# Adding a small constant inside the mask multiplication and not in a pass of its own

## The chip, the cores and the metric

The kernel runs on one core of a Trainium2 chip. Of the engines of the core, TensorE does the matrix products, ScalarE (ACT in the profile) applies functions element by element, VectorE (DVE) does arithmetic on one or two tensors, GpSimd (POOL) does some of the additions, and SyncE (SP) issues nearly all transfers. The metric is the device time of one execution in microseconds (us), the median over several runs.

## The reference

Sixty-four graphs of 256 nodes with 512 features each go through an attention layer with 8 heads and then a graph-attention block with two more attentions. The adjacency matrix `adj` (256 x 256 for each graph) holds edge weights between 0.05 and 1, and zero where there is no edge (about 97 in 100 entries; the diagonal is always set). It enters three times:

```python
# layer 0, 8 heads
scores = Q K^T / sqrt(64) + soul_bias + log(adjacency + 1e-9)
out = softmax(scores) V + x
# layer 1, first 8 heads, then one head
e = leaky_relu(s_i + t_j, 0.2) + bias          # bias is the same adjacency
out = softmax(e) h + x
```

In layer 0, exp(log(a + 1e-9) + z) is (a + 1e-9) exp(z). So the logarithm needs not be taken: the exponentials of the scores are multiplied by the adjacency plus the constant. In layer 1 the adjacency is added to the scores as it is.

## The kernel before

**Layout.** All attention matrices are held turned: a partition is a source node j, and the columns are the target nodes. So the adjacency of a graph is turned first. `turn_adj` in `graph` does it with two VectorE transposes of 128x256 (line 501, called for each half j), from the tile `A` as loaded into `AT`, 128 partitions by 2 x 256 columns. Then one ScalarE pass over the whole of `AT` (128x512, line 517) adds `eps`, a column of 1e-9:

```python
nc.scalar.activation(AT, AT, AF.Identity, bias=eps)
```

**Where `AT` is read.** Layer 0: after the exponentials of the scores (line 599, ScalarE, straight from PSUM into `ET`), VectorE multiplies them by `AT` (line 613). For each graph there are four such passes of 128x1024, for two groups of four heads and the two halves j; `AT` is broadcast over the four heads. After each group of heads the two halves are summed (line 618, `total`), and TensorE sums the columns of the totals for the softmax denominators (line 384 in `weight_sums`). Layer 1, first attention: `AT` is added to the scores (line 682) between two ScalarE passes (lines 676 and 686). Layer 1, last attention: `AT` goes through an exponential in place (line 739) and is a factor in line 744. `AT` has four buffers, since several graphs are under way at once.

**Projections.** Products of 512 features are done by a scheme with seven block products in place of eight, in `winograd` (lines 326 and 333 are its matmuls). They use three PSUM banks, a, b and c, over and over: `m1` is copied out of a and `m5` out of b, then products 2 and 6 follow, then `u2` is copied out of a, products 3, 7 and 4 follow. So a product that goes into bank a again has to wait until the copy of what lay there is done. For K these copies are ScalarE passes (line 525, `m<-ps_a`, `m<-ps_b`, `u<-ps_a` of 128x256).

**Order of the work.** A graph is a generator of 40 or so steps with names ("turn", "Q", "K", "K7", "mask", "weights" and so on). The list `period` says in which order the steps of up to six graphs are taken, and it repeats for each graph; a `start` and a `finish` list stand around it. For TensorE this order is kept as written:

```python
with tc.manual_schedule(engines={mybir.EngineType.PE}):
```

The order of the other engines is left to the framework's planner, which starts from the program order and its own costs. In `period` the steps around the turning are these (the number is how many graphs back):

```python
(0, "turn"), (1, "Q4"), (1, "K"), (1, "K7"), (3, "weights"),
```

At the end a check of the value ranges decides whether a slow, plain path has to be run for some graphs (the loop over `again`); with the inputs here it is not run. It has its own code for the constant and is not touched.

Of the kernel before, what the change touches and what calls it, by code (L numbers as in the profile page):

```python
# [10 lines left out]
AF = mybir.ActivationFunctionType  # L11
ALU = mybir.AluOpType
AX = mybir.AxisListType

P = 128
# [5 lines left out]
def kernel(  # L21
# [24 lines left out]
    nc = tc.nc  # L46
    B, N, D = x.shape
# [11 lines left out]
    eps = const.tile([P, 1], F32, name="eps")  # L59
# [92 lines left out]
    with ExitStack() as main:  # L152
# [324 lines left out]
        def graph(b):  # L477
# [22 lines left out]
            def turn(to, blocks):  # L500
                nc.vector.transpose(to, blocks)
# [7 lines left out]
            AT = data.tile([P, NT, N], F32, name="AT", tag="AT", bufs=4)  # L509

            def turn_adj():
                for j in range(NT):
                    turn(
                        AT[:, j, :].rearrange("p (t a r) -> p a t r", t=NT, a=4),
                        A.rearrange("p (a t) (j r) -> p j a t r", t=NT, j=NT)[:, j],
                    )
                nc.scalar.activation(AT, AT, AF.Identity, bias=eps)

            if b > 0:
                turn_adj()  # L520
# [21 lines left out]
            if b == 0:  # L542
                turn_adj()
# [66 lines left out]
            totals = []  # L610
            for ET, tag in zip(pair, ("QT", "KT")):
                for j in range(NT):
                    nc.vector.tensor_tensor(  # L613
                        ET[:, j, :, :], ET[:, j, :, :],
                        AT[:, j, :].unsqueeze(1).to_broadcast([P, 4, N]), ALU.mult,
                    )
                total = data.tile([P, 4, N], F32, name="total", tag=tag)
                nc.vector.tensor_tensor(total, ET[:, 0], ET[:, 1], ALU.add)
                totals.append(total)
                yield  # L620
# [49 lines left out]
            for q in range(2):  # L670
                ET = work.tile([P, NT, 4, N], F32, name="ET1", tag="ET", bufs=4)
                pair.append(ET)
                for h in range(4):
# [5 lines left out]
                    if h % 2 == 1:  # L679
                        for j in range(NT):  # L680
# [4 lines left out]
                            for i in (h - 1, h):  # L685
                                nc.scalar.activation(  # L686
                                    ET[:, j, i, :], ET[:, j, i, :], AF.Exp,
                                    bias=targets[:, j, 4 * q + i : 4 * q + i + 1],
# [53 lines left out]
            ET = work.tile([P, NT, N], F32, name="ET2", tag="ET2", bufs=1)  # L742
# [115 lines left out]
        graphs = {}  # L858
        with tc.manual_schedule(engines={mybir.EngineType.PE}):
            graphs[0] = graph(0)  # L860
            next(graphs[0])
            wv, wq, wk = weight("wv", 1), weight("wq"), weight("wk")
# [22 lines left out]
            for g, name in order:  # L885
                for key, (behind, t, w) in list(unloaded.items()):
                    if (g, name) == (key, "transpose") or behind in graphs:
                        load_weight(nc.sync, t, w)
                        del unloaded[key]
                if (g, name) == (0, "Q"):  # L890
                    nc.vector.tensor_scalar(wq[:, :, :4], wq[:, :, :4], SCALE, None, ALU.mult)
                    combine(wq)
                if (g, name) == (0, "K"):
                    combine(wk)
                if (g, name) != (0, "load"):
                    if g not in graphs:
                        graphs[g] = graph(g)
                    next(graphs[g])
                if (g, name) == (B - 1, "rows 2"):

                    note_odd(seen[:, : 4 * B], -1.0, 1e25)
                    note_odd(seen[:, 4 * B :], -1.0, 3600.0)
# [13 lines left out]
    with ExitStack() as rest:  # L916
# [6 lines left out]
        def tl(name, *shape):  # L923
            return pool.tile(list(shape), F32, name=name, tag=name)
# [108 lines left out]
        with tc.For_i(0, again) as b:  # L1033
# [8 lines left out]
            eps = tl("eps", P, 1)  # L1042
# [82 lines left out]
```

## Time and profile before

| | |
|---|---|
| median of 3 runs | 3233.33 us (3231.98 to 3235.2) |
| profiled execution, its own time | 3234.22 us |
| its span in the profile | 3232.4 us |
| granted TensorE clock, mean | 0.991 |
| DMA traffic | 407.94 MB, mean 126 GB/s |
| one period (from one L517 to the next, steady stretch) | 48.3 to 49.7 us mostly |

The span is what the profiler saw of the one execution; the execution's own time is 1.8 us longer. Busy shares are averages over the whole span, and the profile's slices show all engines at an even load from the second slice to the last but one. L517 means line 517 of the kernel. "ET<-ET,AT" says which tile is written from which. "x512" is a count. The time in brackets behind a line of the timeline is how long the engine sat idle before it, and what ended that. PE is TensorE's matmuls and PEld its loads of weights.

### The profile page before, as it was taken

Reading aid. Unit: us, or ns where it says so; the run is one execution under the profiler, and the core shown is the slowest. Engines: PE = TensorE matmul, PEld = TensorE weight load, DVE = VectorE, ACT = ScalarE, POOL = GpSimd, SP = SyncE. Lnnn points to the kernel's source line nnn. Section 1 sums busy time; section 2 is a strip of 40 time slices with the busy share of each in tenths; the row PEclk is TensorE's granted clock in tenths of the full one; section 3 lists DMA queues with packets and bytes.
Section 4 is the critical chain, followed back from the end, with each engine's and each line's share of the span. In section 5 each row is a group of like instructions: output and inputs, shape, how many; then the busy total and the mean of one; then the engine's idle time right before and its main releaser. Section 6 shows DMA issues by size and latency. Waiting matters only on the chain. (4 is left out here: it accounts for less than half of the span.)

```text
span 3232.4 us, 77827 instructions
## 1 busy us (share of the span) xinstructions
PE 3135.6 (97%) x28232; PEld 2621.6 (81%) x28232; DVE 2717.1 (84%) x6093; ACT 2188.5 (68%) x5959; POOL 1068.4 (33%) x1315
## 2 busy tenths in 40 slices
PE   7899999999999999999999999999999999999986
PEld 5678888888888888888888888888888888888864
DVE  5788888888888888888888888888888888888885
ACT  3467677677677677676676676676676676676673
POOL 3232332332332332333333333333323423423333
PEclk9999999999999999999999999999999999999998
DMA  4234444444444444444444444444444434444432
GB/s 133 92 118 131 124 131 131 126 127 133 127 128 133 127 124 135 128 122 134 129 122 136 125 126 124 131 130 125 132 124 132 132 123 133 131 123 133 125 116 90
DMA packets 354664, 407.94 MB, mean 126 GB/s; under 512 B 117840, under 2 KB 262496, under 8 KB 354272
## 3 DMA queue, kind: packets, MB, share of 16 engines
q1 hardware_dynamic: 353120, 401.83, 41.6%
q8 instruction: 224, 3.67, 0.5%
q14 instruction: 168, 1.38, 0.1%
q10 hardware_dynamic: 1152, 1.06, 0.1%
HBM read 266.83 MB, written 135.87 MB: 125 GB/s over the span
## 5 line engine op out<-in xcount | busy, mean ns | idle before, releaser
L682 DVE TENSOR_TENSOR ET<-ET,AT 128x512 f32<-128x512 f32 x512 | 363.4, 711 | 239.3 <-ACT ET L676 238.7
L686 ACT ACTIVATE ET<-ET,ends 128x256 f32<-128x256 f32 x1024 | 482.1, 503 | 104.7 <-DVE ET L682 103.6
L676 ACT ACTIVATE ET<-R,f 128x256 f32<-128x256 f32 x1024 | 461.3, 501 | 74.9 <-PE ps_num L425 55.7
L425 PE MATMUL ps_num<-ET,V 128*32 128x256 f32 x8192 | 466.7, 379 | 0.0
L302 POOL TENSOR_TENSOR S<-yT 128x256 f32<-128x256 f32 x64 | 47.7, 746 | 1210.5 <-ACT zT L409 967.6
L765 POOL TENSOR_TENSOR X<-X,weighted 128x256 f32<-128x256 f32 x256 | 210.9, 834 | 545.0 <-ACT weighted L764 536.9
L425 PEld LDWEIGHTS ps_num<-ET,V 128*32 128x32 f32 x8192 | 263.9, 110 | 155.2 <-issue 1.1
L613 DVE TENSOR_TENSOR ET<-ET,AT 128x1024 f32<-128x1024 f32 x256 | 306.6, 1231 | 39.4 <-ACT ET L599 39.4
L599 ACT ACTIVATE ET<-ps_sc,V 128x512 f32<-128x512 f32 x512 | 302.3, 697 | 7.8 <-PE ps_sc L592 7.8
L756 PE MATMUL ps_av<-V,ET 128*128 128x258 f32 (+1 forms) x1024 | 250.7, 389 | 24.3 <-DVE ET L744 24.3
L326 PE MATMUL ps_a<-w,S 128*128 128x264 f32 (+1 forms) x1024 | 268.5, 385 | 4.9 <-ACT m L639 2.9
L326 PE MATMUL ps_b<-w,S 128*128 128x264 f32 (+1 forms) x1024 | 266.6, 383 | 0.8 <-DVE w L131 0.7
L592 PE MATMUL ps_sc<-QT,KT 64*128 64x256 f32 x2048 | 239.4, 383 | 0.0
L263 DVE BATCH_NORM_STATS2 parts<-Z 128x6 f32<-128x128 f32 x1024 | 238.3, 275 | 0.1
L756 PEld LDWEIGHTS ps_av<-V,ET 128*128 128x128 f32 x1024 | 189.8, 196 | 48.9 <-issue 13.0
L326 PEld LDWEIGHTS ps_a<-w,S 128*128 128x128 f32 x1024 | 185.9, 189 | 46.7 <-ACT m L639 6.9
L326 PEld LDWEIGHTS ps_b<-w,S 128*128 128x128 f32 x1024 | 193.8, 189 | 32.5 <-PE ps_a L326 1.1
L592 PEld LDWEIGHTS ps_sc<-QT,KT 64*128 64x128 f32 x2048 | 192.4, 187 | 24.8 <-issue 1.5
L646 ACT ACTIVATE V<-ps_a,rstd 128x257 f32<-128x257 f32 (+1 forms) x128 | 60.0, 469 | 199.2 <-PE ps_a L326 199.2
L434 DVE TENSOR_TENSOR ps_num<-ps_num,R 128x512 f32<-128x512 f32 x256 | 169.9, 687 | 9.6 <-DMA R<-kept 7.0
L702 POOL TENSOR_TENSOR Z<-Z,bw 128x1024 f32<-128x1024 f32 x64 | 175.7, 2745 | 4.1 <-DVE parts L263 3.0
L409 ACT ACTIVATE yT<-yT,columns 128x256 f32<-128x256 f32 x256 | 120.8, 499 | 65.4 <-DMA yT<-kept 65.4
(175 smaller groups left out, 7396.3 us busy)
## 6 DMA issues: line engine op xcount, KB each, us to landing
R<-kept SPq DMA_DIRECT2D x128, 512.0 KB
X<-in_x_dram SPq DMA_DIRECT2D x256, 128.0 KB
kept<-xT SPq DMA_DIRECT2D x64, 512.0 KB
yT<-kept SPq DMA_DIRECT2D x64, 512.0 KB
R<-kept SPq DMA_DIRECT2D x512, 64.0 KB
kept<-yT SPq DMA_DIRECT2D x64, 512.0 KB
kept<-Z SPq DMA_DIRECT2D x64, 512.0 KB
X<-kept SPq DMA_DIRECT2D x512, 64.0 KB
```

The lines of the kernel that those rows point to most:

```text
L263: nc.vector.bn_stats(parts[:, block].rearrange("p h c -> p (h c)"), Z[:, block, :])
L326: nc.tensor.matmul(to, A[:, kk, :], B[:, kk, :], start=(first and kk == 0), stop=(kk == 1), skip_group_check=not first,)
L425: nc.tensor.matmul(num[32 * a : 32 * a + 32, m * N : (m + 1) * N], V[:, j, a // 2, a % 2 * P + q * DH + 32 * m :][:, :32], pair[a // 2][:, ...
L592: nc.tensor.matmul(banks[h % 2][:, o : o + N], KT[lo : lo + DH, (q + h) // 2, j * P : (j + 1) * P], QT[lo : lo + DH, (q + h) // 2, :], sta ...
L599: nc.scalar.activation(ET[:, j, i::2, :], banks[i].rearrange("p (h n) -> p h n", n=N), AF.Exp, bias=c[:, j, :],)
L613: nc.vector.tensor_tensor(ET[:, j, :, :], ET[:, j, :, :], AT[:, j, :].unsqueeze(1).to_broadcast([P, 4, N]), ALU.mult,)
L676: nc.scalar.activation(ET[:, j, h, :], R[q][:, h, :], AF.Relu, bias=f[:, j, at : at + 1])
L682: nc.vector.tensor_tensor(two, two, AT[:, j, :].unsqueeze(1).to_broadcast([P, 2, N]), ALU.add)
L686: nc.scalar.activation(ET[:, j, i, :], ET[:, j, i, :], AF.Exp, bias=targets[:, j, 4 * q + i : 4 * q + i + 1],)
L702: nc.gpsimd.tensor_tensor(Z, Z, folded["2"].row.unsqueeze(1).to_broadcast([P, 2 * KC, P]), ALU.add)
L756: nc.tensor.matmul(av[:, :width], ET[:, j, t * P : (t + 1) * P], V2[:, j, n, :width], start=(j == 0), stop=(j == NT - 1),)
L765: nc.gpsimd.tensor_tensor(o[:, cols], o[:, cols], weighted, ALU.add)
```

## The change

`turn_adj` no longer adds the constant; `AT` holds the adjacency as it was loaded, only turned. The four mask passes of layer 0 become a scalar-tensor-tensor with two operations: the constant 1e-9, given in the instruction, is added to `AT`, and the sum is multiplied by the exponentials. In layer 1 the adjacency is now used without the constant, as in the reference.

```diff
                         AT[:, j, :].rearrange("p (t a r) -> p a t r", t=NT, a=4),
                         A.rearrange("p (a t) (j r) -> p j a t r", t=NT, j=NT)[:, j],
                     )
-                nc.scalar.activation(AT, AT, AF.Identity, bias=eps)
 
             if b > 0:
                 turn_adj()
...
             for ET, tag in zip(pair, ("QT", "KT")):
                 for j in range(NT):
-                    nc.vector.tensor_tensor(
-                        ET[:, j, :, :], ET[:, j, :, :],
-                        AT[:, j, :].unsqueeze(1).to_broadcast([P, 4, N]), ALU.mult,
+                    nc.vector.scalar_tensor_tensor(
+                        ET[:, j, :, :], AT[:, j, :].unsqueeze(1).to_broadcast([P, 4, N]), 1e-9,
+                        ET[:, j, :, :], ALU.add, ALU.mult,
                     )
                 total = data.tile([P, 4, N], F32, name="total", tag=tag)
                 nc.vector.tensor_tensor(total, ET[:, 0], ET[:, 1], ALU.add)
```

## The prediction

> **What bounds the kernel now.** I read the engine totals first, then the waits of TensorE, then one period of each engine's timeline. The totals:
>
> ```profile
> PE 3135.6 (97%) x28232; PEld 2621.6 (81%) x28232; DVE 2717.1 (84%) x6093; ACT 2188.5 (68%) x5959; POOL 1068.4 (33%) x1315
> ```
>
> TensorE is busy throughout. The groups that it works through follow each other at a constant distance, so time can be lost or won only where that distance is larger than usual. Its waits outside the start and the end are few; the largest that recurs is one on a ScalarE copy:
>
> ```profile
> PE ps_av L756 <- DVE ET L744: 24.3, 4, 12.6
> PE ps_a L333 <- ACT m L525: 16.4, 27, 1.7
> ```
>
> The first of these is the tail (4 waits, up to 12.6 us). The second is the K projection of the middle of a period. ScalarE and TensorE there, from the timeline (start, length, and in brackets the idle time before):
>
> ```profile
> 1537.18 0.60 ACT L558 ACTIVATE QT<-ps_a,columns 128x128 f32<-128x128 f32 x2
> 1537.68 0.36 ACT L525 COPY m<-ps_a 128x256 f32<-128x256 f32 x1
> 1537.93 0.38 ACT L525 COPY m<-ps_b 128x256 f32<-128x256 f32 x1
> 1538.19 0.52 ACT L686 ACTIVATE ET<-ET,ends 128x256 f32<-128x256 f32 x1
> 1538.61 0.72 ACT L517 ACTIVATE AT<-AT,eps 128x512 f32<-128x512 f32 x1
> 1539.22 0.51 ACT L686 ACTIVATE ET<-ET,ends 128x256 f32<-128x256 f32 x1
> 1539.62 0.36 ACT L525 COPY u<-ps_a 128x256 f32<-128x256 f32 x1
> ```
>
> ```profile
> 1538.09 1.16 PE L333 MATMUL ps_a<-S,wk 128*128 128x128 f32 x8 [0.54 <-ACT m L525]
> 1539.08 1.06 PE L333 MATMUL ps_b<-S,wk 128*128 128x128 f32 x8
> 1540.03 1.16 PE L333 MATMUL ps_a<-S,wk 128*128 128x128 f32 x8
> ```
>
> The pass that goes (L517) stands behind both m copies and ahead of the u copy. I compared its neighbours in all 64 repeats: in the steady stretch they are these every time, about 48.3 to 49.7 us from one L517 to the next. So L517 cannot cause the wait on m; it can only hold up u, which product 7 (the third group above) needs.
>
> **What the Trainium skill says.**
> - "Perfetto Trace Analysis", section "Identifying the Most-Contended Engine": matmul busy time is no good measure of a full TensorE, because matmuls overlap; weight-load busy time is one. Here that is 81%, so I count distances between starts and not the 97%.
> - "ScalarE: Activation LUTs", "What ACT_TABLE_LOAD costs": a pass with a per-partition bias takes 280 ns + 0.833 ns per element, and neighbours overlap by about 93 ns. For 512 elements 707 ns; the trace has 720, and the next pass starts 0.61 us after L517. It agrees.
> - "VectorE: DVE Perf Modes", "The TRN2 errata": an fp32 tensor_tensor takes (N+151)/0.96 ns, for 1024 elements 1224; L613 has a median of 1225. It agrees.
> - "Vector Engine (DVE) Microarchitecture Reference", "Points that are easy to get wrong": a scalar-tensor-tensor with two non-bf16 SBUF sources runs at half throughput. The trace disagrees: L744 is such an instruction, and 256 elements take 474 ns, not over 530.
>
> **Removed.** 64 passes of L517: 46.1 us of ScalarE by the table of groups, about 64 x 0.61 = 39 us of its queue. What that is worth to TensorE:
> - Steady stretch. From product 3 to product 7 of K takes 1540.03 - 1539.08 = 0.95 us; the same step of Q (1527.28 to 1528.17) takes 0.89. I read it in 56 periods between 250 and 3000 us: 54 have 0.05 to 0.07 too much, and the sum is 3.5 us. Without L517 ScalarE reaches u at 1539.62 - 0.61 = 1539.01, but u then waits for product 6 (end 1538.09 + 1.16 = 1539.25). It would end near 1539.66, before product 3 has been fed (1539.08 + 0.89 = 1539.97). So all of the 0.06 goes: 57 x 0.06 = 3.4 us. Lower end 0, if another pass (L676, step 0.40) fills the gap. The rest of the 0.61 us is worth nothing: ScalarE idles again at 1543.03 and 1545.36 for TensorE and VectorE, which is where it is absorbed.
> - Start. Twice TensorE waits on a copy that stands behind L517, which itself waits for the turning on VectorE:
>
> ```profile
> 44.12 1.14 PE L326 MATMUL ps_a<-wv,S 128*128 128x257 f32 x4 [1.14 <-ACT u L525]
> 97.20 1.16 PE L326 MATMUL ps_a<-w,S 128*128 128x264 f32 x4 [1.43 <-ACT u L639]
> ```
>
>   The first 1.14 us is given back at 68.81, where TensorE waits 3.51 us for the folded weights, which start on GpSimd at 61.46 after 20.2 us that the profile puts down to issue and not to TensorE. After the second, the next group waits on V (L648), at 98.40 on VectorE. It stands behind L537, which ends its turn at about 98.2; so 0.2 us is left of 1.43. I take 0.2, ends 0 and 2.5.
>
> **Added.** Each of the 256 mask passes (L613) becomes a scalar-tensor-tensor with an immediate, over the same 1024 elements. No such pass of that size is in the trace. The prices that bound it:
>
> ```profile
> L613 DVE TENSOR_TENSOR ET<-ET,AT x256: 1206/1225/1792, 38.9 to 3120.9; 128x1024 f32<-128x1024 f32 x128
> L744 DVE SCALAR_TENSOR_TENSOR ET<-R,f,AT x126: 466/474/947, 221.6 to 3202.3; 128x256 f32<-128x256 f32 x126
> L374 DVE SCALAR_TENSOR_TENSOR bad<-seen 128x256 f32<-128x256 f32 x2 | 0.8, 414 | 0.0
> L374 DVE SCALAR_TENSOR_TENSOR bad<-seen 128x128 f32<-128x128 f32 x2 | 0.6, 281 | 0.0
> ```
>
> L374 takes an immediate: (414-281)/128 = 1.04 ns per element and 148 ns fixed, so 1024 elements give about 1214 ns, 11 less than L613. L744, whose scalar is a column, costs 474-414 = 60 more. At two elements the form with an immediate (L288) and the plain one (L289) both average 149. I take +-0; ends -11 and +60, and 1067 more if the halving did apply.
>
> This price matters, because the mask chain is tight. VectorE starts it at 1511.08, does six passes (four L613, two L618) and ends at 1518.15; TensorE's column sums (L384) start at 1518.27. The same 0.11 to 0.14 us lies between the two in 58 of 63 periods. A wake-up takes 0.05 (m ends 1538.04, TensorE starts 1538.09), so the slack is about 0.075 us: 19 ns per pass. Beyond it each ns costs 4 x 57 = 0.23 us. At +60: 57 x (0.24 - 0.075) = 9.4 us. At -11 at most 57 x 0.044 = 2.5 us is won. GpSimd is idle from 1511.4 to 1530, so it does not disturb the passes.
>
> **Moved.** AT's last writer is now VectorE's turning. L613 and L682 follow it on their own engine, and L739 comes a whole period later, so no wait is added; no DMA is touched. Only TensorE's order is written by hand. The trace shows passes of the other engines out of program order (L409 between the L367s at 1520 to 1522), so the planner may arrange ScalarE and VectorE anew around the hole.
>
> **Sum.** The profiled execution took 3234.2 us (span 3232.4), 0.9 above the median. 3.4 + 0.2 = 3.6 us less is 3230.6 profiled, 3229.7 at the median; with 0.7 of the 2.5 that shorter masks could give I say 3229. This case's own range: 3225 (3.4 + 2.5 + 2.5 won) to 3233 (nothing won).
>
> **Rivals.** Two thousandths are 6.5 us, about what a measurement of this kernel can tell from no change.
> - *Likeliest, 0.49*: the order holds and only u profits. 0.33 of this within the bound, 0.16 faster than it, when the small gains add up.
> - *The wait on m shrinks, 0.22*: it loses 25.2 us over 57 periods above the usual distance, of which 57 x 0.09 = 5 come with any such change of group; 20 can be had. If the planner moves a pair of L686 behind m, half of it goes: 3233.3 - 3.6 - 12 = about 3218; all of it, 3210. For: an emptier ScalarE. Against: 26 late arrivals of R (18.9 us of ScalarE waiting for the DMA) seem to start this wait, and they do not change.
> - *A pass in front of m, 0.19, slower*: the new order puts one more L676 or L686 (0.40 us) ahead of the m copy, and TensorE waits that much longer in each period: 57 x 0.40 - 3.6 = 19 more, 3252; in half of the periods 3241. It decides from (6.5 + 3.6)/57 = 0.18 us per period on. For: this copy already has no slack in most periods. Against: the hole comes after m, and ScalarE is idle again 4 us later.
> - *The new pass is longer, 0.08*: +60 ns gives 3229.7 + 9.4 = 3239 (0.04, inside the bound); above 63 ns it is slower than the bound, and at half throughput 57 x (4.27 - 0.075) = 239 more, near 3470 (0.04). Against: L744 and L374.
> - *Nothing moves, 0.02*: the freed time is hidden, 3233.
>
> **Range and chances.** Faster 0.16 + 0.22 = 0.38; within 0.33 + 0.04 + 0.02 = 0.39; slower 0.19 + 0.04 = 0.23. From 3215 to 3243: below lies about a third of the second case (0.07), above half of the third (0.10) and the long masks (0.03). The tail, 3140 us on, waits for chains on VectorE and DMA; I count no gain there.
>
> **What would show it.** ScalarE's busy time falls by 46 us to about 2142; L613 stays at 1214 to 1235 ns; product 3 to 7 of K takes 0.89; the waits at 44 and 97 us are gone and the one at 68.8 is longer. I am wrong if the ScalarE order around K differs, if the wait on m changes by more than 5 us in sum, or if L384 gains a wait on L618.

## The result and the profile after

| | before | after |
|---|---|---|
| median of 11 runs each, us | 3235.2 (3231.45 to 3241.38) | 3245.76 (3239.05 to 3251.89) |
| ratio, 95% interval | | 1.0034 (1.0026 to 1.0041) |
| span of the profiled execution, us | 3232.4 | 3243.9 |
| granted TensorE clock | 0.991 | 0.991 |

The kernel became 10.6 us slower, where 4 us faster was forecast. The 64 passes are gone all the same. The engine totals of the changed kernel:

```profile
PE 3140.4 (97%) x28232; PEld 2621.1 (81%) x28232; DVE 2720.0 (84%) x6093; ACT 2153.9 (66%) x5895; POOL 1067.7 (33%) x1315
```

ScalarE has 64 instructions less and 34.6 us less busy time. From here on, lines behind 517 stand one lower than before (L613 is now L612, and so on). The mask pass in its new form, from the view by tile (shortest/median/longest in ns):

```profile
L612 DVE SCALAR_TENSOR_TENSOR ET<-AT,ET x256: 1207/1225/1785, 39.3 to 3131.0; 128x1024 f32<-128x1024 f32 x128
```

Its median is the 1225 ns of the plain multiplication, so the added form costs no more than the old one. Where time is lost is seen in the waits of TensorE:

```profile
PEld ps_a L333 <- ACT m L524: 27.1, 45, 2.0
PE ps_a L333 <- ACT m L524: 17.9, 27, 1.8
PEld ps_a L333 <- ACT u L524: 15.8, 59, 0.3
```

The columns are total us, number of waits, longest. The two waits on m are those of before, hardly changed (24.8 and 16.4 us then). The third is new: 59 times, once in nearly every period, TensorE waits up to 0.3 us for the copy of u. The same place on ScalarE and on TensorE, from the timeline of the changed kernel (L675 are Relu passes and L685 Exp passes, two of each for every head, one for each half j; the three groups of TensorE are products 6, 3 and 7):

```profile
1542.16 0.36 ACT L524 COPY m<-ps_a 128x256 f32<-128x256 f32 x1
1542.41 0.38 ACT L524 COPY m<-ps_b 128x256 f32<-128x256 f32 x1
1542.68 0.92 ACT L685 ACTIVATE ET<-ET,ends 128x256 f32<-128x256 f32 x2
1543.49 0.91 ACT L675 ACTIVATE ET<-R,f 128x256 f32<-128x256 f32 x2
1544.28 0.36 ACT L524 COPY u<-ps_a 128x256 f32<-128x256 f32 x1
```

```profile
1542.57 1.16 PE L333 MATMUL ps_a<-S,wk 128*128 128x128 f32 x8 [1.28 <-ACT m L524]
1543.57 1.06 PE L333 MATMUL ps_b<-S,wk 128*128 128x128 f32 x8
1544.70 1.16 PE L333 MATMUL ps_a<-S,wk 128*128 128x128 f32 x8
```

Before, L686, L517, L686 stood between the second m copy and the u copy. The hole that L517 left has been filled with two Relu passes (L675, 128x256, x2), which before came right after u, as the timeline of the kernel before has it:

```profile
1539.87 0.92 ACT L676 ACTIVATE ET<-R,f 128x256 f32<-128x256 f32 x2
```

From the second m copy to u it was 1539.62 - 1537.93 = 1.69 us and is now 1544.28 - 1542.41 = 1.87. What u copies, product 6, ends at about 1542.57 + 1.16 = 1543.73; u could start there, 0.55 us earlier, but the two Relu passes stand ahead of it on ScalarE. So product 7 (1544.70) begins 1.13 us after product 3 (1543.57), where 0.95 was needed before. The same step takes 0.89 in the Q projection and, further down, in kernels in which u is early.

Summed over the periods between 250 and 3000 us, this one step is 13.5 us above 0.893 (56 periods), against 3.5 before (57 periods): 10.0 us more, where the medians differ by 10.6 (8.4 to 13.3 by the interval). The order on ScalarE, read for all 64 repeats, has the two Relu passes ahead of u in 60 of them, and before in one. Apart from these 59 pairs and the 64 passes that are gone, ScalarE's order is that of before. The order of TensorE, VectorE, GpSimd and SyncE is the same as before, instruction by instruction, apart from the changed form of the mask passes.

At the start 1.9 us was won (the first of the regular column sums in layer 0 begins at 250.82 and not at 252.69). By the end, the corresponding sums are 10.1 us late (3133.07 and 3123.00). So the regular stretch between the two lost 11.9, most of it at this step. The start, from the timeline of TensorE:

```profile
68.40 2.02 PE L200 MATMUL ps_fold<-w,left 128*32 128x264 f32 x10 [4.12 <-ACT left L195]
98.65 1.45 PE L326 MATMUL ps_a<-w,yT 128*128 128x264 f32 x4 [2.05 <-DVE V L647]
```

The waits at 44 and 97 us are gone, and the ones shown here have grown in their place, from 3.51 to 4.12 us and from 0.59 to 2.05. Of the 1.9 us, most is chance: in the profiled execution of the kernel before, the granted clock is 0.57 between 136 and 140 us, and two groups of projection matmuls take 3.39 us (136.49 to 139.88); in the changed kernel it is 1.00 there, and the same two groups take 1.73 (135.86 to 137.59).

### The profile page after: what moved, and what is told of

It is laid out like the page before. It is cut to its first block, busy times and chain, and to the rows that moved or that the text cites. A ratio compares the mean times of both kernels' runs of the same rounds, so it can differ in the third digit from the quotient of the medians.

```text
span 3243.9 us, 77763 instructions
## 1 busy us (share of the span) xinstructions
PE 3140.4 (97%) x28232; PEld 2621.1 (81%) x28232; DVE 2720.0 (84%) x6093; ACT 2153.9 (66%) x5895; POOL 1067.7 (33%) x1315
## 4 chain that ended last, share of the span: by engine, by line
PE 67%; ACT 17%; DMA 7%; DVE 4%; SPq 1%; issue 1%; POOL 0%; DVEq 0%
PE ps_a L326 20%; PE ps_b L326 10%; PE ps_av L755 7%; PE ps_sc L591 7%; PE ps_a L333 7%; ACT ET L675 6%; PE ps_num L425 6%; PE ps_c L326 5%; ACT ET L685 5%; DMA R<-kept 5%; PE ps_su L384 3%; PE ps_b L333 2%; ACT zT L409 1%; DVE inverse L390 1%; DVE ET L681 1%; DMA zT<-kept 1%
## 5 line engine op out<-in xcount | busy, mean ns | idle before, releaser
L685 ACT ACTIVATE ET<-ET,ends 128x256 f32<-128x256 f32 x1024 | 475.9, 503 | 104.9 <-DVE ET L681 103.9
L675 ACT ACTIVATE ET<-R,f 128x256 f32<-128x256 f32 x1024 | 467.6, 500 | 76.5 <-PE ps_num L425 55.8
L612 DVE SCALAR_TENSOR_TENSOR ET<-AT,ET 128x1024 f32<-128x1024 f32 x256 | 306.7, 1231 | 39.6 <-ACT ET L598 39.6
L326 PE MATMUL ps_a<-w,S 128*128 128x264 f32 (+1 forms) x1024 | 268.0, 384 | 3.3 <-ACT m L638 2.7
L326 PE MATMUL ps_b<-w,S 128*128 128x264 f32 (+1 forms) x1024 | 266.6, 383 | 0.6 <-DVE w L131 0.5
L326 PEld LDWEIGHTS ps_a<-w,S 128*128 128x128 f32 x1024 | 186.0, 189 | 44.1 <-ACT m L638 6.2
L326 PEld LDWEIGHTS ps_b<-w,S 128*128 128x128 f32 x1024 | 193.7, 189 | 32.3 <-PE ps_a L326 0.9
L763 ACT ACTIVATE weighted<-ps_av,rinv 128x256 f32<-128x256 f32 x256 | 114.4, 471 | 115.2 <-DVE rinv L760 99.6
```

Of the source, the lines that this page charges most:

```text
L326: nc.tensor.matmul(to, A[:, kk, :], B[:, kk, :], start=(first and kk == 0), stop=(kk == 1), skip_group_check=not first,)
L612: nc.vector.scalar_tensor_tensor(ET[:, j, :, :], AT[:, j, :].unsqueeze(1).to_broadcast([P, 4, N]), 1e-9, ET[:, j, :, :], ALU.add, ALU.mult,)
L675: nc.scalar.activation(ET[:, j, h, :], R[q][:, h, :], AF.Relu, bias=f[:, j, at : at + 1])
L685: nc.scalar.activation(ET[:, j, i, :], ET[:, j, i, :], AF.Exp, bias=targets[:, j, 4 * q + i : 4 * q + i + 1],)
```

## The experiments

The question was what loses 10 us: the longer form of the mask instruction, or the new order on ScalarE; and in the second case, which instruction in which place. All ratios are to the kernel before, run beside it on the same chip (5 to 21 runs of each new kernel), with their 95% intervals.

### The two halves of the change apart

`e1_both`: the new mask passes, and the ScalarE pass kept, but adding a column of zeros (the constant is then added only in the mask passes).

```diff
+    none = const.tile([P, 1], F32, name="none")
+    nc.gpsimd.memset(none, 0.0)
...
-                nc.scalar.activation(AT, AT, AF.Identity, bias=eps)
+                nc.scalar.activation(AT, AT, AF.Identity, bias=none)
...
-                    nc.vector.tensor_tensor(
-                        ET[:, j, :, :], ET[:, j, :, :],
-                        AT[:, j, :].unsqueeze(1).to_broadcast([P, 4, N]), ALU.mult,
+                    nc.vector.scalar_tensor_tensor(
+                        ET[:, j, :, :], AT[:, j, :].unsqueeze(1).to_broadcast([P, 4, N]), 1e-9,
+                        ET[:, j, :, :], ALU.add, ALU.mult,
```

> The masks are the new ones (scalar-tensor-tensor with 1e-9), and the ScalarE pass over the turned adjacency is kept, but adds a zero. The planned order of ScalarE is then that of the kernel before, with the pass between the m and the u copy of K and both Relu passes behind u. Theory A (the loss comes from the new order alone, two Relu passes ahead of u): same as before, ratio 1.000, 3235 us; product 3 to product 7 of K takes 0.95 us. Theory B (the longer mask instruction or its waits cost the time): as the changed kernel, ratio 1.0033, 3246 us.

`e2_neither`: the mask passes as before, and the ScalarE pass taken out. The constant 1e-9 is thereby left out of the computation.

```diff
-                nc.scalar.activation(AT, AT, AF.Identity, bias=eps)
```

> The ScalarE pass is taken out and the masks stay plain tensor-tensor multiplications; the constant 1e-9 is left out of the computation. The planned order of ScalarE is that of the changed kernel. Theory A (order): as the changed kernel, ratio 1.0033, 3246 us, product 3 to 7 of K 1.14 us. Theory B (mask instruction): faster than before by the pass taken out, 3232 us, ratio 0.999.

Measured: `e1_both` 3238.57 against 3238.98 us, 1.0002 (0.9994 to 1.0010), and the order on every engine is that of before (with one memset more at the start). `e2_neither` 3249.11, 1.0031 (1.0020 to 1.0042), and the order on every engine is that of the changed kernel. So the new form of the mask costs nothing that can be measured, and the whole loss comes with taking the pass out.

### The pass kept, only moved behind u

If the place of u in the queue is the cause, then the loss must appear without removing anything. `e8_pass_behind_u` is the kernel before, with the pass and its constant kept, only issued behind the u copy of its own graph's K. (`issue_after` tells the planner that an instruction may not be placed ahead of another; it is an order, and not a wait on data.)

```diff
-                nc.scalar.activation(AT, AT, AF.Identity, bias=eps)
...
-            for _ in winograd(left, wk, False, copy, put_k):
+            copies = {}
+
+            def copy_k(d, s, row, column):
+                copies[row, column] = nc.scalar.copy(d, s).ins
+
+            for _ in winograd(left, wk, False, copy_k, put_k):
                 yield
+            with tc.issue_after(copies[0, 1]):
+                nc.scalar.activation(AT, AT, AF.Identity, bias=eps)
```

> The kernel before, masks and pass over the turned adjacency and all, with this pass only issued behind the u copy of K of its own graph. The planner then puts the two Relu passes ahead of u, as in the changed kernel. Theory A (the place ahead of u is what counts, not what was removed or added): slower than before with no work changed, product 3 to 7 of K 1.14 us, ratio 1.003, 3246 us. A theory in which taking the pass out of ScalarE's queue in front of u is a gain (the working of the prediction): 3.5 us faster, ratio 0.999.

Measured: 3248.28 against 3237.68 us, 1.0034 (1.0021 to 1.0047). ScalarE of this kernel:

```profile
1545.19 0.92 ACT L692 ACTIVATE ET<-ET,ends 128x256 f32<-128x256 f32 x2
1546.00 0.90 ACT L682 ACTIVATE ET<-R,f 128x256 f32<-128x256 f32 x2
1546.80 0.36 ACT L583 COPY u<-ps_a 128x256 f32<-128x256 f32 x1
...
1548.66 0.72 ACT L588 ACTIVATE AT<-AT,eps 128x512 f32<-128x512 f32 x1
```

No instruction is added or taken away, and yet it has the same pair of Relu passes (here L682) ahead of u, the same 1.13 us from product 3 to product 7, and the same loss. Apart from the 64 passes behind u, its order is that of the changed kernel on every engine. What is lost is due to the order alone.

### u put ahead of the Relu passes again

`e3_u_first` is the changed kernel with the Relu passes of the heads 6 and 7 held behind the u copy. `e4_one_ahead` has the condition `(0, 1) if (at, j) >= (6, 1) else None` in the same place, and so lets one Relu of head 6 go ahead of u. Against the changed kernel, both differ in nothing but the order of u and these Relu passes on ScalarE.

```diff
+        def after_copy(which):
+            return tc.issue_after(copies[which]) if which in copies else nullcontext()
...
-            for _ in winograd(left, wk, False, copy, put_k):
+            def copy_k(d, s, row, column):
+                copies[row, column] = nc.scalar.copy(d, s).ins
+
+            for _ in winograd(left, wk, False, copy_k, put_k):
...
-                        nc.scalar.activation(
-                            ET[:, j, h, :], R[q][:, h, :], AF.Relu, bias=f[:, j, at : at + 1]
-                        )
+                        with after_copy((0, 1) if at >= 6 else None):
+                            nc.scalar.activation(
+                                ET[:, j, h, :], R[q][:, h, :], AF.Relu, bias=f[:, j, at : at + 1]
+                            )
...
+        copies = {}
```

> The changed kernel with one thing added: the Relu passes of heads 6 and 7 may be issued only behind the u copy of K, so that no Relu pass stands ahead of u. Theory A: product 3 to 7 of K takes 0.89 us, which is 0.25 less than in the changed kernel in each of 57 periods, 14 us: 3232 us, ratio to before 0.999 (3.5 us less). If the lost time has another place (the wait on m, the start): 3246 us still, ratio 1.0033.

> As the one before, but one Relu pass (head 6, first half) stays ahead of u, and not two. Theory A in numbers: behind m5 at 1537.93 come two Exp passes and one Relu (3 x 0.40), u ends near 1539.78, before product 3 has been fed (1539.97): no loss, 3232 us, product 3 to 7 at 0.89. A rival in which each Relu pass ahead of u costs its 0.40 or half of the loss: 3239 us, ratio 1.001.

`e9_pass_and_relu_behind_u` does the same to `e8_pass_behind_u`: the pass is kept, behind u, and so are the Relu passes of the heads 6 and 7.

> As the one before, and the Relu passes of heads 6 and 7 behind u too, so that only two Exp passes stand between m5 and u; the pass over the adjacency is still done. Theory A: product 3 to 7 at 0.89 us, as fast as the changed kernel with u first, ratio to before 0.998. If the 64 passes cost something of their own beyond their place, it stays between: 0.999 to 1.000.

Measured: `e3_u_first` 3232.21 against 3238.98 us, 0.9979 (0.9972 to 0.9986). `e4_one_ahead` 3230.78, 0.9976 (0.9969 to 0.9983). `e9_pass_and_relu_behind_u` 3233.05 against 3237.68, 0.9985 (0.9978 to 0.9991). The step from product 3 to 7 takes 0.89 in all three. The step in question, side by side: its median, its sum over 0.893 us in the 56 or 57 periods between 250 and 3000 us, and the length of the regular stretch of the profiled execution, from the first to the last regular column sums:

| kernel | passes from the m copies to u | product 3 to 7, us | sum over 0.893, us | regular stretch, us | ratio |
|---|---|---|---|---|---|
| before | Exp, pass, Exp | 0.950 | 3.5 | 2870.3 | 1 |
| after | Exp x2, Relu x2 | 1.135 | 13.5 | 2882.2 | 1.0034 |
| `e1_both` | Exp, pass, Exp | 0.953 | 4.3 | 2872.0 | 1.0002 |
| `e2_neither` | Exp x2, Relu x2 | 1.136 | 13.6 | 2883.2 | 1.0031 |
| `e8_pass_behind_u` | Exp x2, Relu x2 | 1.135 | 13.5 | 2882.1 | 1.0034 |
| `e3_u_first` | Exp x2 | 0.893 | 0.0 | 2868.1 | 0.9979 |
| `e4_one_ahead` | Exp x2, Relu | 0.893 | 0.0 | 2867.4 | 0.9976 |
| `e9_pass_and_relu_behind_u` | Exp x2 | 0.893 | 0.0 | 2868.0 | 0.9985 |

The two traces with the same order, before and `e1_both`, differ by 1.7 us in the regular stretch, so smaller differences there say little. With one Relu ahead nothing is lost; with two, 0.185 us more per period than before. It is a threshold and not a price per pass: a rival that put a cost on each Relu ahead of u fell with `e4_one_ahead`. What the 64 passes themselves are worth lies between `e9_pass_and_relu_behind_u`, which has them, and `e3_u_first`, which doesn't. The ratios differ by 0.0006, about 2 us, which their intervals don't tell from nothing (0.9978 to 0.9991, 0.9972 to 0.9986), and in the traces the regular stretch is equally long in both. So with u free, removing the passes won nothing there that can be measured: the gain of the steady stretch comes from the place of u, and not from the removal.

### More passes behind the copies

The wait on m costs more than u does: product 2 to product 6 takes 25.1 us over 0.893 each in the changed kernel, summed as above, and 23.9 before. Since ScalarE's queue ahead of m holds Relu passes too, three kernels held more of them back: `e5_all_behind` (condition `(0, 1) if at >= 4 else None`), `e6_before_behind` (the same on the kernel before, with the pass kept) and `e7_half_behind` (`(1, 1) if at == 5 else (0, 1) if at >= 6 else None`, where `(1, 1)` is the second m copy).

> The changed kernel, with the Relu passes of all four heads of the second group (4 to 7) allowed only behind the u copy of K. ScalarE no longer sits in front of the m copies waiting for the transfer of R and then working through four Relu passes. If the wait on m comes from these passes, it falls from 26.4 us in sum over the usual distance of groups to about 5 (56 x 0.09), and with u free as well the time is 14 + 20 us less than the changed kernel: 3212 us, ratio to before 0.992. If ScalarE then becomes late for what follows (the Exp passes of heads 4 to 7 come some 4 us later), part of it is given back: ratio 0.995 or more, with a new wait of TensorE after the K stage.

> The kernel before, with the same rule for the Relu passes of heads 4 to 7 and the pass over the turned adjacency kept. The planner then puts this pass between the two m copies. If order is all that counts and the pass itself is harmless, as fast as the changed kernel with this rule, ratio to before 0.992. If the pass costs its queue time here, because m5 and u now stand right behind it: u ends near 0.6 us later than without it, up to 0.2 to 0.6 us per period of TensorE's time, 11 to 34 us: ratio 0.995 to 1.002.

> The changed kernel with the Relu passes of head 5 behind m5 and those of heads 6 and 7 behind u; head 4 stays in front of m. The wait on m loses two of the four Relu passes (0.8 us of queue) but keeps the wait for the transfer of R. If the four passes make the wait, it shrinks as with all behind, ratio 0.992 to 0.994; if the late transfer makes it, it stays above 15 us in sum, ratio 0.996 to 0.998. Two Relu passes stand ahead of u again, but with no Exp pass there, so u is not late.

All three were far off: 3449.56 against 3241.23 us, 1.0633 (1.0607 to 1.0659); 3458.61, 1.0660 (1.0638 to 1.0683); 3347.96, 1.0331 (1.0310 to 1.0352). The wait on m did fall (to 4.3, 3.1 and 7.9 us), but new waits came up. In `e5_all_behind`, from the waits:

```profile
PE ps_a L326 <- DVE V L653: 139.4, 64, 2.3
PE ps_a L326 <- ACT m L644: 29.9, 64, 2.5
```

VectorE and GpSimd of that kernel at one of the 64 places of the first kind, from the timeline:

```profile
1599.56 2.14 DVE L265 TENSOR_TENSOR parts<-parts 128x16 f32<-128x16 f32 x1
1601.62 0.48 DVE L653 SCALAR_TENSOR_TENSOR V<-ps_a,rstd,m 128x264 f32<-128x264 f32 x1
```

```profile
1599.32 2.34 POOL L708 TENSOR_TENSOR Z<-Z,bw 128x1024 f32<-128x1024 f32 x1 [3.84 <-DVE parts L263]
```

With the Relu passes late, the planner also arranged VectorE and the transfers anew. An addition of 16 columns (L265), which takes 184 ns in the median, took 2.14 us and ended (1601.70) when GpSimd's addition (1601.66) did; and behind it in the queue was a pass that writes V, which TensorE waited for. The kernel before has the same slow addition about once per period (2.38 us at 1501.98), but nothing behind it that TensorE is short of. 64 waits of 2.2 us make 139 us, where 208 are lost in all; the rest was not taken apart. In `e7_half_behind` the largest new wait of the matmuls is that on a reciprocal on VectorE (L767, 41.2 us in 59 waits), and the next is on the u copy of Q (30.5 us in 58).

`e10_one_behind_m` holds back less: two Relu heads behind u as in `e3_u_first`, and a single Relu behind the second m copy.

```diff
-                        with after_copy((0, 1) if at >= 6 else None):
+                        with after_copy((1, 1) if (at, j) == (5, 1) else (0, 1) if at >= 6 else None):
```

> The changed kernel with u first (heads 6 and 7 behind u), and of the four Relu passes of heads 4 and 5 the last one allowed only behind m5; it takes 0.40 us of queue from in front of the m copies. If the wait on m can be had in small pieces: it falls from 28 us in sum to below 15, 3221 to 3225 us, ratio 0.994 to 0.996. If moving these passes breaks the order further down, as it did with two and four of them: slower than before, ratio above 1.005, with a wait of TensorE on VectorE or on the Q copies.

Measured: 3223.49 against 3237.68 us, 0.9955 (0.9943 to 0.9967), faster than both kernels. From its timeline, ScalarE and TensorE around K:

```profile
1530.18 0.36 ACT L584 COPY m<-ps_a 128x256 f32<-128x256 f32 x1
1530.43 0.52 ACT L692 ACTIVATE ET<-ET,ends 128x256 f32<-128x256 f32 x1
1530.84 0.36 ACT L584 COPY m<-ps_b 128x256 f32<-128x256 f32 x1
1531.09 0.52 ACT L682 ACTIVATE ET<-R,f 128x256 f32<-128x256 f32 x1
1531.50 0.51 ACT L692 ACTIVATE ET<-ET,ends 128x256 f32<-128x256 f32 x1
1531.90 0.37 ACT L584 COPY u<-ps_a 128x256 f32<-128x256 f32 x1
```

```profile
1530.64 1.11 PE L333 MATMUL ps_a<-S,wk 128*128 128x128 f32 x8
1531.58 1.06 PE L333 MATMUL ps_b<-S,wk 128*128 128x128 f32 x8
1532.48 1.06 PE L333 MATMUL ps_a<-S,wk 128*128 128x128 f32 x8
```

One Relu now stands behind both m copies that stood ahead of them, one Exp has come between the two, and one of the two Q passes ahead of them goes earlier. The matmul into bank a follows without a recorded wait, and product 7 follows product 3 after 0.90. The wait on m is 7.0 us, where `e3_u_first` has 28.6. That is about 22 us less at this place, but the regular stretch is only 11.0 shorter (2857.1 and 2868.1): TensorE is held elsewhere for the rest. The trace names one such place: weight loads of L326 wait for the m and u copies of layer 1's V projections (15.2 and 14.5 us, 6.8 and 8.1 in `e3_u_first`). The profiled spans (3227.0 and 3220.7) differ by 6.3, since the start of this execution took 4.6 us longer.

## Why the prediction was wrong

**Right, by its own steps.** That TensorE's distances decide, and that the place to look at is product 3 to 7 of K, held up by u. That `AT` without the pass adds no wait: the loads of the column sums wait for the totals (L384 for L618, now L617) 61 times, 23.4 us in sum, before and after. That the mask passes cost nothing: 1225 ns before and after, and `e1_both` at 1.0002; the rivals of +60 ns and of half throughput are out. That the wait on m stays (23.9 and 25.1 us by the count used here). That the waits at 44 and 97 us go and the one at 68 grows. A changed order of ScalarE around K, which it named as a sign of being wrong, is what came.

**The step that failed** is the one on the regular stretch: "So all of the 0.06 goes: 57 x 0.06 = 3.4 us. Lower end 0, if another pass (L676, step 0.40) fills the gap." The filling was named, but with one pass. Two came, 0.80 us for a hole of 0.61, and u began 0.18 us later after the second m copy, where the working had it end about 0.3 earlier. Product 3 to 7 took 1.135 us and not 0.89. That turned a gain of 3.4 us into a loss of 10.0 at this step; 57 x 0.185 gives 10.5. The lower end of 0 was the mistake in the working: the number of passes that could fill the hole was bounded by nothing but what stood behind u, and the trace showed two Relu passes there (1539.87, x2). With both, the sum would have given a bound: (0.80 - 0.61) x 57 = 11 us lost. The likeliest case rested on "the order holds"; the prediction says that the planner may arrange ScalarE anew around the hole, but counts a loss from a further pass only in front of m.

**The slower rival** had the right mechanism in the wrong place. It put an extra pass in front of m, at 0.40 us per period; two passes came in front of u, at 0.185. Its objection, that the hole comes after m, was sound for m, and was the very reason to look at u.

**Sizes.** ScalarE's busy time was to fall by 46 us and fell by 34.6: in the trace each of the 64 passes shares 0.10 us with the pass before it and 0.10 with the one behind, so only 33 of the 46 us are its own. The start was to give 0.2 us and gave 1.9, within its ends of 0 and 2.5, but by luck: the group that waits for V starts at 98.65, 0.3 earlier than before, which is the size forecast, and 1.7 more is the lower clock of one execution of the kernel before. In the rival on the wait on m, half of 20 us is 10 and not 12, which makes 3220. And its 5 us that "come with any such change of group" are no fixed cost: in `e10_one_behind_m` product 2 to 6 takes 0.894 in the median, where it never took less than 0.979 before.

**Where the forecast holds.** With u's place kept, `e3_u_first` has the forecast 0.89 at the step, and its median is 6.8 us less where 3.6 were forecast. The size agrees in part only. In its trace the regular stretch is 2.2 us shorter, and not 3.4: the wait on m is 4.6 us longer (28.6 and 23.9). The start is 5.4 us shorter (first regular column sums at 247.28), and about 3.3 of that are matmuls that the kernel before did at a lower granted clock in its profiled execution (0.66 from 98 to 103 us and 0.57 from 136 to 140, against 1.00 in both places). The rest was not taken apart.

**Open.** Why the planner fills the hole with two Relu passes can't be seen in any trace, since the traces show its order and not its costs. That it does so when the pass is removed and also when it is only moved behind u is what `e2_neither` and `e8_pass_behind_u` show.

## What to carry to other kernels

Where a planner orders the queues, taking an instruction out of one can also change what follows it: here the hole was filled by whole instructions, and overfilled. Before a removal is costed, mark each instruction in that queue that the bound engine waits for, and add up the ready passes that could slip in ahead of it. Then pin the few copies that matter by an explicit order, as few as will do: here one or two rules on Relu passes won 0.2 to 0.45%, and holding back one to three passes more lost 3.3 to 6.6%.

## What the runs showed of the hardware

- A scalar-tensor-tensor with an immediate over 128x1024 fp32, both tensors in SBUF, takes 1225 ns, as the plain multiplication does. The page "Vector Engine (DVE) Microarchitecture Reference" of the Trainium skill ("Points that are easy to get wrong") says that such a pair of sources halves the throughput; the measurement decides.
- A copy late by 0.2 us in each period showed in full at the end: 10.0 us at the one step, 11.9 in the regular stretch, 10.6 in the medians. With TensorE's order fixed and its groups at constant distances, nothing made up for it. The opposite doesn't hold: of the 22 us taken from the wait on m, 11 arrived in the stretch.
- An addition of 16 columns on VectorE (L265) takes 0.17 to 2.4 us. In the kernel before, 60 of the 128 take 1.7 us or more, and every one of them ends within 0.05 us of an addition of 128x1024 on GpSimd (L702) that had begun 0.4 to 1.0 us before it; `e5_all_behind` has 60 such cases too (begun 0.2 to 1.0 us before).
